# A gated cross-attention and expert layer on one Trainium2 core: first batch projected ahead of the branch, heads' products pinned

## The chip, the core and the metric

The kernel runs on one core of a Trainium2 chip. A core has TensorE (PE in the profile; PEld is its weight load), VectorE (DVE), ScalarE (ACT), GpSimd (POOL), and SyncE (SP), which here only issues transfers and waits for them. Transfers are issued by an engine into a queue and carried by 16 DMA engines. The metric is the device time of one execution in microseconds (us), with all inputs and outputs in the chip's memory. The time before is 850.95 us, the median of three runs (848.28 to 854.89).

## What is computed

The input x has 8 batches of 512 tokens of 256 numbers, the context likewise. Attention has 16 heads of 16 numbers. The feed-forward part has 8 experts with an inner size of 1,024; each token goes to its best two. The reference, cut to what matters:

```python
q = query @ wq.T + bq;  k = key @ wk.T + bk;  v = value @ wv.T + bv
scores = einsum('bhqd,bhkd->bhqk', q, k) / sqrt(16)
attn = softmax(where(mask == 0, -1e9, scores))
xattn = einsum('bhqk,bhkd->bhqd', attn, v) @ wo.T + bo
...
probs = softmax(x_flat @ router_w + router_b);  top_w, top_idx = top_k(probs, 2)
output += comb[:, e] * (gelu(x_flat @ expert_up[e].T) @ expert_down[e].T)   # for each expert e
...
x = x + tanh(g_xattn) * xattn(layernorm(x), ctx, ctx, mask)
x = x + tanh(g_ffn) * ffn(layernorm(x))
```

The mask is 512 x 512 integers, the same for all batches and heads. In the inputs drawn here every row is the same and keeps only the keys at the end, at most 128 of the 512.

## The kernel before

*Two branches, one mask.* The kernel handles any mask, but has a fast branch for masks whose kept keys lie within 128 neighbouring places, the same in every row. Whether that holds is found on the chip. The mask comes in four parts (L96 to L100, SP's queue). DVE turns each into 0 and 1 (`dropped`, L286), PE sums over the queries (`n_ps`, L292), DVE marks the keys that are kept (`act`, L293), and `most` (L298), a product and a maximum in one instruction, finds the first kept key, the end of the kept keys, and whether the rows differ (L303 to L305). From the first key comes the window's place `window_i`; from all three comes the flag `near_i` (L309 to L313). Then DVE makes, from the window, the matrix `pick` (L320 to L333) that PE uses to transpose the keys and blank those not kept, and the scaled biases `bks`, `bkm`, `bqs` and the value buffers `vals` (L336 to L349). All engines read `near_i` and branch (L1309); in the fast branch, `attend_near` (L718), SP also reads `window_i` (L741) and loads the window of the first two batches' context and the second batch's x.

*What is loaded when.* SP's queue takes x of batch 0 (L85), the mask, then the attention weights (L244 to L251). ACT's queue takes nine small inputs (L123 to L133): the two gates, five biases, the router's weights, and `bv` spread over all partitions. On DVE, small preparations (`iota_e` to `less`, L142 to L270) stand in the built order ahead of the comparisons with the mask; so does the first layernorm's statistics, `measure` (L207).

*One batch of attention.* Scores are made against 128 keys. The heads lie on partitions in pairs: 32 rows of a tile hold two heads of 16, and a tile of 128 rows holds four such pairs; there are two tiles, c = 0 and 1, and i = 0 and 1 chooses one of each pair. `k` holds the keys twice, with one head of each pair at zero (`half`), so that a product over 32 rows is one head's scores. The steps, for (c, i) = (0,0), (0,1), (1,0), (1,1), which are the four groups of a batch:
- `find_tops` (L834): eight products of 32 rows, `t_ps`, into four banks of PSUM; DVE takes each query's maximum over the keys.
- `lower_tops` (L851): PE transposes the maxima and DVE puts them, negated by way of `km`, into the spare rows of the queries (`lowered`, the tile `ql`).
- `weights_T` (L863): four products of 32 rows, one for each pair of heads, `w_ps`, into four banks; ACT takes the exponential into `pT`. This gives the softmax's weights with keys on partitions.
- `weigh` (L880): four products of 128 x 32 into one bank, `n_av`; DVE transposes and divides by the sums (L884 to L893).
- `project_out` (L900): the output projection, added to x.

`km` is the keys once more, with another bias (`bkm`, which is `bks` and `less` together) that puts -1 in the rows where the maxima come. Both `k` and `km` are made by ACT from the bank `k_ps` (L799 to L806), with four activations of 128 x 128 each.

*The order of the work.* Batch b's `weights_T` and `weigh` run beside batch b+1's `find_tops` and beside the preparation of batch b+2 (its projections `kv_ps`, `k_ps`, `q_ps`, L787 to L818), the layernorm statistics of batch b+3, and the routing of batch b-1. This is written out by hand. `between` (L915 and on) gives each step a place (g, n): group g of four, slot n of three. The loop over b from -1 to 7 runs the slots in order. A table (`amid`) puts the first experts' work into the slots of batches 4 to 7; the other experts' products follow, on PE alone. A tile scheduler decides how instructions that are not pinned to each other stand on an engine; `tc.keep_in_program_order` pins an instruction behind the last one before it in the program on its engine. In the built order of before, other instructions stand between the products of a group in 15 groups of `w_ps` and 7 of `t_ps`.

The statistics of batch 1 are computed ahead of the loop, those of batch 2 in the slots of b = -1. Buffers: four banks of PSUM for `t_ps` and `w_ps` (`ps_s`), two for projections and transposes (`bank`), two for `n_av`.

Of the kernel before, what the change touches and what calls it, by code (L numbers as in the profile page):

```python
# [10 lines left out]
F32 = mybir.dt.float32  # L11
I32 = mybir.dt.int32
# [7 lines left out]
P = 128  # L20
# [43 lines left out]
def flamingo_layer(ctx: ExitStack, tc: tile.TileContext, a: dict, out: bass.AP):  # L64
# [19 lines left out]
    def load_x(b, pool=keep):  # L84
        xs[b] = pool.tile([P, QT, D], F32, tag="x", name=f"x{b}", bufs=5 if b else 1)  # L85
        nc.sync.dma_start(out=xs[b], in_=token_rows(a["x"], b))


    load_x(0)
# [12 lines left out]
    mask_i = load_mask(mk)  # L102
    bq = fixed([P, DC], "bq")
# [18 lines left out]
    for dst, src in (  # L122
        (gates[:, 0:1], a["g_xattn"].partition_broadcast(P)),  # L123
        (gates[:, 1:2], a["g_ffn"].partition_broadcast(P)),
        (bk, a["bk"]),
        (bq, a["bq"]),
        (bvT, a["bv"].rearrange("(c p) -> p c", p=P)),
        (bo, a["bo"].partition_broadcast(P)),
        (rb, a["rb"].partition_broadcast(P)),
        (rw[:, :, :E], a["rw"].rearrange("(c p) e -> p c e", p=P)),  # L130
        (bv, a["bv"].partition_broadcast(P)),
    ):
        nc.scalar.dma_start(out=dst, in_=src)  # L133
# [10 lines left out]
    nc.scalar.activation(tg, gates, AF.Tanh)  # L144
# [99 lines left out]


    load_w("wqT")
    wkv = fixed([P, DC, 2 * D], "wkv")
    for i, n in enumerate(("wkT", "wvT")):
        nc.sync.dma_start(out=wkv[:, :, i * D : (i + 1) * D], in_=a[n].rearrange("(c p) d -> p c d", p=P))
        w[n] = wkv[:, :, i * D : (i + 1) * D]  # L250
    load_w("woT")  # L251

    own = fixed([P, 1], "own")
    tc.keep_in_program_order(nc.vector.tensor_copy(own, own_i))
    keys = mk.tile([P, S], F32, tag="keys", name="keys")
    tc.keep_in_program_order(nc.vector.tensor_copy(keys, keys_i))

    ahead = mk.tile([P, 2, S], F32, tag="ahead", name="ahead")
    tc.keep_in_program_order(nc.vector.tensor_scalar(ahead[:, 0, :], keys, -1.0, float(S), ALU.mult, ALU.add))
    tc.keep_in_program_order(nc.vector.tensor_scalar(ahead[:, 1, :], keys, 1.0, None, ALU.add))  # L260

    less = fixed([P, 2], "less")
    ident_j = ident.rearrange("p (j i) -> p i j", i=2 * DH)
    for i in range(2):
        tc.keep_in_program_order(nc.vector.tensor_reduce(less[:, i : i + 1], ident_j[:, DH * i, :], AX.X, ALU.add))
    tc.keep_in_program_order(nc.vector.tensor_scalar(less, less, -1.0, None, ALU.mult))  # L270

    act = mk.tile([P, S], F32, tag="act", name="act")
    first = fixed([P, 1], "first")
    window = fixed([P, 1], "window")
    window_i = fixed([P, 1], "window_i", I32)
    near_i = fixed([P, 1], "near_i", I32)
    with early, tc.tile_pool(name="ps_mask", bufs=1, space=PSUM) as ps_mask:

        def column(name, n=1):
            return mk.tile([P, n], F32, tag=name, name=name)  # L280

        dropped = mk.tile([P, QT, S], BF16, tag="dropped", name="dropped")
        norms_0 = measure(const, [(0, "a")], True)
        norms_0[1][0]()
        for t in range(QT):
            ins = nc.vector.tensor_scalar(dropped[:, t, :], mask_i[:, t, :], 0.0, None, ALU.is_equal)  # L286
            tc.keep_in_program_order(ins)
        norms_0[2]()

        n_ps = ps_mask.tile([P, S], F32, tag="n", name="n_ps")  # L290
        for t in range(QT):
            nc.tensor.matmul(n_ps, lhsT=ones_b, rhs=dropped[:, t, :], start=(t == 0), stop=(t == QT - 1))  # L292
        nc.vector.tensor_scalar(act, n_ps, float(S), None, ALU.is_lt)  # L293
        junk = column("junk", S)
        uneven, end = column("uneven"), column("end")

        def most(src, dst):
            nc.vector.tensor_tensor_reduce(  # L298
                junk, src, act, scale=1.0, scalar=0.0, op0=ALU.mult, op1=ALU.max, accum_out=dst
            )  # L300

        most(ahead[:, 0, :], first)
        nc.vector.tensor_scalar(first, first, -1.0, float(S), ALU.mult, ALU.add)  # L303
        nc.vector.tensor_scalar(window, first, float(S - WINDOW), None, ALU.min)
        tc.keep_in_program_order(nc.vector.tensor_copy(window_i, window))  # L305
        most(ahead[:, 1, :], end)
        most(n_ps, uneven)
        near = column("near")
        nc.vector.tensor_tensor(near, end, first, ALU.subtract)  # L309
        nc.vector.tensor_scalar(near, near, float(WINDOW), None, ALU.is_le)  # L310
        nc.vector.scalar_tensor_tensor(near, end, 1.0, near, ALU.is_ge, ALU.mult)
        nc.vector.scalar_tensor_tensor(near, uneven, 0.0, near, ALU.is_le, ALU.mult)
        tc.keep_in_program_order(nc.vector.tensor_copy(near_i, near))  # L313

        kept = fixed([P, 1], "kept")
        here = fixed([P, 1], "here")
        tc.keep_in_program_order(nc.vector.tensor_scalar(here, own, window, None, ALU.add))  # L320
        eq = column("eq", S)
        nc.vector.tensor_scalar(eq, keys, here, None, ALU.is_equal)
        nc.vector.tensor_tensor_reduce(eq, eq, act, scale=1.0, scalar=0.0, op0=ALU.mult, op1=ALU.max, accum_out=kept)
        diag = column("diag", P)
        nc.vector.tensor_scalar(diag, ident, kept, None, ALU.mult)
        row_ps = ps_mask.tile([P, P], F32, tag="row", name="row_ps")
        nc.tensor.matmul(row_ps, lhsT=ones, rhs=diag, start=True, stop=True)
        lead = fixed([P, 1], "lead")
        nc.vector.tensor_tensor(lead, here, first, ALU.is_equal)
        drop = column("drop", P)  # L330
        nc.vector.tensor_scalar(drop, row_ps, -1.0, 1.0, ALU.mult, ALU.add)
        pick = fixed([P, P], "pick")
        nc.vector.scalar_tensor_tensor(pick, drop, lead, diag, ALU.mult, ALU.add)  # L333


        vals = [fixed([P, H, 2 * DH], f"nv{i}") for i in range(3)]  # L336
        for t in vals:
            nc.vector.memset(t[:, :, DH:], 1.0)
            nc.vector.tensor_scalar(t[:, :, DH:], t[:, :, DH:], kept, None, ALU.mult)

        bks = fixed([P, 2, DC], "bks")
        for i in range(2):
            ins = nc.vector.tensor_scalar(bks[:, i, :], bk, half[:, 1 - i : 2 - i], None, ALU.mult)
            tc.keep_in_program_order(ins)
        bkm = fixed([P, 2, DC], "bkm")
        for i in range(2):
            nc.vector.tensor_scalar(bkm[:, i, :], bks[:, i, :], less[:, i : i + 1], None, ALU.add)
        bqs = fixed([P, DC], "bqs")
        tc.keep_in_program_order(nc.vector.tensor_scalar(bqs, bq, 1.0 / DH**0.5, None, ALU.mult))  # L349


    def shared(p2, small, bank):
# [145 lines left out]
        return layernorms, finish  # L498

# [219 lines left out]
    def attend_near(att):  # L719
# [18 lines left out]
        def held(shape, name, dtype=F32):  # L738
            return hold.tile(shape, dtype, tag=name, name=name)

        at = nc.values_load(  # L741
            window_i[0:1, 0:1], engines=(mybir.EngineType.SP,), min_val=0, max_val=S - WINDOW,
            skip_runtime_bounds_check_because="it is the lesser of the first key and S - WINDOW",
        )
        wins = {}

        def load_win(b):
            t = p2.tile([P, DC, WINDOW], F32, tag="win", name=f"win{b}", bufs=3)
            nc.sync.dma_start(
                out=t, in_=a["ctxT"][b].rearrange("(c p) s -> p c s", p=P)[:, :, bass.ds(at, WINDOW)]  # L750
            )
            wins[b] = t

        for b in range(2):
            load_win(b)
            if b == 0:
                load_x(1, p2)
# [14 lines left out]
        made = {}  # L772

        def prepare(b):

            xnT[b] = p2.tile([P, DC, S], F32, tag="xnT", name=f"n_xnT{b}", bufs=1)
            q = p2.tile([P, DC, S], F32, tag="q", name=f"n_q{b}")
            k = p2.tile([P, DC, 2, WINDOW], F32, tag="k", name=f"n_k{b}")
            km = p2.tile([P, DC, 2, WINDOW], F32, tag="km", name=f"n_km{b}")
            v = vals[b % 3]  # L780
            made[b] = (q, k, km, v)
            said = {}

            def keys_values():
                ps = bank(f"kv_ps{b}")
                for dc in range(DC):
                    nc.tensor.matmul(  # L787
                        ps, lhsT=wins[b][:, dc, :], rhs=wkv[:, dc, :], start=(dc == 0), stop=(dc == DC - 1)
                    )
# [590 lines left out]
```

## Time and profile before

One execution was profiled. It is a run of its own beside the three timed ones.

| | |
|---|---|
| median of three runs | 850.95 us |
| the profiled execution | 849.25 us |
| its span in the trace | 847.5 us |
| mean granted TensorE clock | 0.972 of full speed |
| moved in the span | 121.58 MB, 143 GB/s |

The page divides the span into 40 equal slices of 21.2 us; each digit is a share in tenths. In rows of a timeline the first number is the start in us from the span's start, the second the duration, then the engine, the line, the operation, the output tile and its inputs, the shape, and how many instructions the row holds; "[2.90 <-DMA mask_i]" says that the engine idled 2.90 us before and that a transfer into `mask_i` ended it. Slices further on look like this: from slice 5 to 19 attention on all engines, with the experts' first transfers; from about 400 us on, the expert products on PE with little beside them but ACT's gelu, and transfers.

```profile
ACT  0544464654455424352411011111112112111210
POOL 2002105252644232545464534444342523434332
DMA  4800011110482313061846566656567576657511
```

ACT and POOL are not full anywhere; DMA is busy in the first two slices, which hold the mask, x and the weights, and again in the experts' part.

### The profile page before, as it was taken

What the parts mean: (1) busy time and instruction counts of PE and PEld (TensorE: products, weight loads), DVE (VectorE), ACT (ScalarE), POOL (GpSimd) and SP (SyncE); (2) the same over time, 40 slices, a digit from 0 to 9 for tenths busy, and PEclk for the clock granted to TensorE, in tenths of its full rate; (3) what the DMA queues carried; (4) which work ended last, traced back from release to release, by engine and by line L of the source; (5) the groups of instructions that cost most, each with busy time, mean ns of one, the idle gap of its engine ahead of it and who ended that gap; (6) DMA issues with size and microseconds to landing.
All of it is one profiled execution on the core that took longest, in us unless ns stands there. A gap on an engine that the chain in (4) does not pass through costs nothing. (4 is left out here: it accounts for less than half of the span.)

```text
span 847.5 us, 11313 instructions
## 1 busy us (share of the span) xinstructions
PE 779.8 (92%) x4090; PEld 574.0 (68%) x4090; DVE 316.2 (37%) x960; ACT 259.4 (31%) x501; POOL 313.9 (37%) x422
## 2 busy tenths in 40 slices
PE   1698999999999899999999799999999999999992
PEld 0343444444356575767788588888898888989882
DVE  7367778787775628435230111111111111011110
ACT  0544464654455424352411011111112112111210
POOL 2002105252644232545464534444342523434332
PEclk9979999999799989999999899999999999999997
DMA  4800011110482313061846566656567576657511
GB/s 137 264 2 7 7 50 34 52 58 22 133 282 90 99 51 114 15 200 52 262 136 205 190 208 189 231 187 223 174 233 238 172 240 233 204 203 255 199 50 36
DMA packets 87909, 121.58 MB, mean 143 GB/s; under 512 B 16797, under 2 KB 71712, under 8 KB 87840
## 3 DMA queue, kind: packets, MB, share of 16 engines
q1 hardware_dynamic: 74448, 93.68, 33.3%
q0 software_dynamic: 11840, 26.76, 10.2%
q8 instruction: 36, 0.59, 0.3%
q10 hardware_dynamic: 1552, 0.28, 0.2%
q14 instruction: 33, 0.27, 0.1%
HBM read 101.05 MB, written 20.17 MB: 143 GB/s over the span
## 5 line engine op out<-in xcount | busy, mean ns | idle before, releaser
L665 PE MATMUL o_ps<-down,hT 128*128 128x256 f32 x1088 | 245.0, 384 | 6.5 <-DVE y L668 6.1
L647 PE MATMUL h_ps<-xT,up 128*128 128x256 f32 (+1 forms) x1152 | 246.6, 372 | 4.8 <-DVE tops L838 3.4
L647 PEld LDWEIGHTS h_ps<-xT,up 128*128 128x128 f32 x1152 | 210.7, 192 | 34.8 <-DVE tops L838 4.2
L665 PEld LDWEIGHTS o_ps<-down,hT 128*128 128x128 f32 x1088 | 206.4, 192 | 38.1 <-DVE y L668 6.3
L651 ACT ACTIVATE hT<-h_ps 128x512 f32<-128x512 f32 (+1 forms) x144 | 82.2, 573 | 363.0 <-PE h_ps L647 362.8
L668 DVE SCALAR_TENSOR_TENSOR y<-o_ps,listed,y 128x256 f32<-128x256 f32 x68 | 32.7, 483 | 277.6 <-DMA y<-out,listed 155.4
L619 POOL DMA_INDIRECT y<-out,listed x68 | 66.1, 972 | 163.1 <-DMA out<-y,listed 124.4
L671 POOL DMA_INDIRECT out<-y,listed x68 | 68.8, 1012 | 100.5 <-DVE y L668 70.5
L838 DVE TENSOR_REDUCE tops<-t_ps 128x4 f32<-128x512 f32 x128 | 79.3, 681 | 34.2 <-PE t_ps L834 34.2
L867 ACT ACTIVATE n_pT<-w_ps 128x512 f32<-128x512 f32 x128 | 70.0, 599 | 68.1 <-PE w_ps L863 68.0
L619 POOL DMA_INDIRECT xg<-rows,listed x68 | 64.9, 954 | 40.8 <-issue 17.4
L863 PE MATMUL w_ps<-ql,n_km 32*128 32x512 f32 x256 | 71.8, 667 | 2.5 <-DVE tops L838 2.5
L489 POOL DMA_INDIRECT table<-entries,place_i x64 | 62.5, 977 | 25.7 <-issue 16.5
L637 DVE COPY xT<-x_ps 128x512 f32<-128x512 f32 (+1 forms) x36 | 23.6, 656 | 101.4 <-PE x_ps L635 101.4
L834 PE MATMUL t_ps<-n_k,n_q 32*128 32x256 f32 x512 | 47.3, 411 | 2.0 <-ACT n_pT L867 1.2
L821 POOL TENSOR_TENSOR x<-x,bo 128x1024 f32<-128x1024 f32 x8 | 18.8, 2363 | 75.1 <-issue 38.8
L834 PEld LDWEIGHTS t_ps<-n_k,n_q 32*128 32x128 f32 x512 | 28.1, 188 | 24.2 <-issue 14.8
L814 PE MATMUL q_ps<-n_xnT,wqT 128*128 128x512 f32 x64 | 34.6, 667 | 6.2 <-ACT n_q L818 3.9
L863 PEld LDWEIGHTS w_ps<-ql,n_km 32*128 32x128 f32 x256 | 23.6, 189 | 21.0 <-DVE tops L838 14.5
L880 PE MATMUL n_av<-n_pT,nv 128*32 128x512 f32 x256 | 36.7, 630 | 0.0
L885 DVE STREAM_TRANSPOSE raw<-n_av 128x512 f32<-128x512 f32 x32 | 22.8, 712 | 35.2 <-PE n_av L880 35.2
L900 PE MATMUL proj_ps<-woT,oT 128*128 128x256 f32 x128 | 32.9, 392 | 1.6 <-DVE oT L893 1.6
(188 smaller groups left out, 547.2 us busy)
## 6 DMA issues: line engine op xcount, KB each, us to landing
up<-in_upT SPq DMA_DIRECT2D x36, 1024.0 KB, 7.7
down<-in_downT SPq DMA_DIRECT2D x36, 1024.0 KB, 6.3
x<-in_x SPq DMA_DIRECT2D x8, 512.0 KB, 4.9
out<-x SPq DMA_DIRECT2D x8, 512.0 KB, 3.0
rows<-xn_f SPq DMA_DIRECT2D x8, 512.0 KB, 3.8
table<-none SPq DMA_DIRECT2D x1, 2288.0 KB, 11.6
xg<-rows,listed POOLq DMA_INDIRECT x68, 3.9
y<-out,listed POOLq DMA_INDIRECT x68, 2.8
```

Of the source, the lines that this page charges most:

```text
L489: nc.gpsimd.indirect_dma_start(out=table_parts[2 * t + i][:, :], out_offset=bass.IndirectOffsetOnAxis(ap=place_i[:, t, i : i + 1], axis=0) ...
L619: nc.gpsimd.indirect_dma_start(out=dst, out_offset=None, in_=src[: seen[JOBS[s][0]], :], in_offset=bass.IndirectOffsetOnAxis(ap=listed[:, ...
L647: nc.tensor.matmul(ps[:, i, :n], lhsT=up[:, dc, (f + i) * P : (f + i + 1) * P], rhs=xT[:, dc, :n], start=(dc == 0), stop=(dc == DC - 1),)
L651: nc.scalar.activation(made[s][:, f : f + 2, :n], ps[:, :, :n], AF.Gelu)
L665: nc.tensor.matmul(ps, lhsT=hT[:, f, h * P : (h + 1) * P], rhs=down[:, f, :], start=(f == 0), stop=(f == FC - 1))
L671: nc.gpsimd.indirect_dma_start(out=out_parts[h][:, :], out_offset=bass.IndirectOffsetOnAxis(ap=listed[:, n, h, 0:1], axis=0), in_=y[:, h, ...
L814: nc.tensor.matmul(ps, lhsT=w["wqT"][:, dc, c * P : (c + 1) * P], rhs=xnT[b][:, dc, :], start=(dc == 0), stop=(dc == DC - 1),)
L834: nc.tensor.matmul(ps[j][:, u], lhsT=q[rows_j, c, t * P : (t + 1) * P], rhs=k[rows_j, c], start=True, stop=True)
L838: nc.vector.tensor_reduce(top[:, 2 * tp : 2 * tp + 2, :].rearrange("p t (i x) -> p t i x", i=2)[:, :, :, 32 * j], ps[j], AX.X, ALU.max,)
L863: nc.tensor.matmul(ps[j], lhsT=km[rows_j, c, i, :], rhs=lowered[b, c][rows_j, i, :], start=True, stop=True)
L867: nc.scalar.activation(pT[:, j, :], ps[j], AF.Exp)
L880: nc.tensor.matmul(av[32 * j : 32 * j + 32, :], lhsT=made[b][3][:, 8 * c + 2 * j + r, :], rhs=pT[:, j, :], start=True, stop=True,)
```

## The change

What it does, by parts:

1. Queues. The mask's four loads are the first on SP's queue; x of batch 0 goes to ACT's queue, with only `bk` and `bq` behind it. The seven other small loads go to SP's queue, behind the first window's load, pinned.
2. The mask's path. The first two comparisons are pinned ahead of the look at batch 0's statistics, the other two behind it. SP reads `window_i` as soon as it is made and loads the first window, ahead of `pick` and of the flag. `end`, `uneven` and `near_i` are computed behind `pick`, the biases and `vals[0]`. The zeros and ones of `vals` are set early.
3. Batch 0's projections (`kv_ps`, `k_ps`, `q_ps`), its scaling and its turns are made ahead of the branch, whatever the mask, with PSUM banks of their own. The window of batch 0 lives in the pool that is given back at the branch. `q`, `k` and `km` become two fixed buffers each, used in turn. The tanh of the gates moves behind these.
4. `km` is made from `k`, not from `k_ps`: two activations of 128 x 256 that add `less`, pinned, placed at slot (3,0).
5. The products of `t_ps`, `w_ps` and `n_av` are pinned, so that nothing stands between those of a group.
6. Statistics of batch 2 move from the slots of b = -1 to (0,0) and (0,1) of b = 0. `keys_values` of batch 1 moves from slot (0,0) to (0,2).

In the built order of after no group of `t_ps`, `w_ps` or `n_av` is cut; apart from the start, PE's instructions stand as before.

The diff, cut to its core (the pinning of `w_ps` and `n_av` reads like that of `t_ps`; the loops over loads name only the tiles):

```diff
-    def load_x(b, pool=keep):
+    def load_x(b, pool=keep, queue=nc.sync):
...
-        nc.sync.dma_start(out=xs[b], in_=token_rows(a["x"], b))
-    load_x(0)
+        queue.dma_start(out=xs[b], in_=token_rows(a["x"], b))
...
     mask_i = load_mask(mk)
+    load_x(0, queue=nc.scalar)
...
-    for dst, src in (gates, gates, bk, bq, bvT, bo, rb, rw, bv):
-        nc.scalar.dma_start(out=dst, in_=src)
+    nc.scalar.dma_start(out=bk, in_=a["bk"])
+    nc.scalar.dma_start(out=bq, in_=a["bq"])
...
-    nc.scalar.activation(tg, gates, AF.Tanh)
...
+        tc.keep_in_program_order(nc.vector.tensor_copy(window_i, window))
+        at = nc.values_load(window_i[0:1, 0:1], engines=(mybir.EngineType.SP,), ...)
+        win = load_window(mk, 0)
+        for dst, src in (gates, gates, bvT, bo, rb, rw, bv):
+            tc.keep_in_program_order(nc.sync.dma_start(out=dst, in_=src))
+        norms_0[2]()
...
+            def keys_less():
+                for i in range(2):
+                    ins = nc.scalar.activation(km[:, :, i, :], k[:, :, i, :], AF.Identity, bias=less[:, i : i + 1])
+                    tc.keep_in_program_order(ins)
...
+        def made_of(b):
+            return qs[b % 2], ks[b % 2], kms[b % 2], vals[b % 3]
+        xnT_0 = mk.tile([P, DC, S], F32, tag="xnT", name="n_xnT0")
+        _, scales, turns = shared(mk, const, bank_0)[0]([(0, "a", xnT_0)], True, norms_0)[2][0]
+        keys_values, keys_T, keys_less, queries = project(0, mk, bank_0, xnT_0, win)
+        for step in (*scales, keys_values, *turns, keys_T, *queries, keys_less):
+            step()
+        tc.keep_in_program_order(nc.scalar.activation(tg, gates, AF.Tanh))
...
-        for b in range(2):
-            load_win(b)
-            if b == 0:
-                load_x(1, p2)
+        load_win(1)
+        load_x(1, p2)
...
-                for dst, bias in ((k, bks), (km, bkm)):
-                    for i in range(2):
-                        for c in range(DC):
-                            nc.scalar.activation(dst[:, c, i, :], ps[...], AF.Identity, bias=bias[...], scale=half[...])
+                for i in range(2):
+                    for c in range(DC):
+                        nc.scalar.activation(k[:, c, i, :], ps[...], AF.Identity, bias=bks[...], scale=half[...])
...
-                    nc.tensor.matmul(ps[j][:, u], ...)
+                    ins = nc.tensor.matmul(ps[j][:, u], ...)
+                    tc.keep_in_program_order(ins)
...
-                put(0, 0, keys_values)
+                put(0, 2 if new == 1 else 0, keys_values)
                 put(0, 1, *scales)
                 put(1, 1, *turns, keys_T)
+                put(3, 0, keys_less)
...
+            if b == 0:
+                looks, settle = normalize((2, "a", lambda: xnT[2]))
+            plan = between(*(n if 0 <= n < B and (b, n) != (-1, 2) else None for n in (b - 1, b + 2, b + 3)))
+            if b == 0:
+                plan[0, 0] += looks
+                plan[0, 1].insert(0, settle)
```

## The prediction

> **What bounds the kernel now.** The page first: span, busy shares, slices.
>
> ```profile
> span 847.5 us, 11313 instructions
> PE 779.8 (92%) x4090; PEld 574.0 (68%) x4090; DVE 316.2 (37%) x960; ACT 259.4 (31%) x501; POOL 313.9 (37%) x422
> PE   1698999999999899999999799999999999999992
> PEclk9979999999799989999999899999999999999997
> ```
>
> TensorE is busy 92% of the span. Only the first slices are not full, and the clock row sags in a few. So two things can be won: the time before PE is full, and PE time that does no work. Next the timeline, all engines, from the start.
>
> ```profile
> 7.60 0.73 DVE L286 TENSOR_SCALAR dropped<-mask_i 128x512 bf16<-128x512 int32 x2
> ...
> 12.87 0.43 DVE L286 TENSOR_SCALAR dropped<-mask_i 128x512 bf16<-128x512 int32 x1 [2.90 <-DMA mask_i<-in_mask]
> ...
> 17.75 0.15 DVE L305 CAST window_i<-window 128x1 int32<-128x1 f32 x1
> ...
> 22.27 0.39 SPq L749 DMA_DIRECT2D win<-in_ctxT  x1
> ...
> 25.01 3.63 PE L787 MATMUL kv_ps<-wkv,win 128*128 128x512 f32 x4 [3.66 <-DMA win<-in_ctxT]
> ...
> 38.57 1.15 PE L834 MATMUL t_ps<-n_k,n_q 32*128 32x256 f32 x16
> ```
>
> A chain of waits: the last mask part (12.87), the window's place (17.90), the branch (22.27), the window's columns (25.01), batch 0's projections (38.57). Then PE's timeline in the steady state; a row is start, length, operation.
>
> ```profile
> 142.95 1.12 PE L863 MATMUL w_ps<-ql,n_km 32*128 32x512 f32 x2
> 144.00 0.71 PE L799 MATMUL k_ps<-pick,kn 128*128 128x128 f32 x4
> 144.55 0.60 PE L851 MATMUL top_ps<-ident,tops 128*128 128x128 f32 x4
> 145.08 1.13 PE L863 MATMUL w_ps<-ql,n_km 32*128 32x512 f32 x6
> 146.15 1.06 PE L880 MATMUL n_av<-n_pT,nv 128*32 128x512 f32 x8
> ```
>
> The two records of one head's 32-row product take 1.05 us (to 144.00), the six of the other three 1.07: heads on different rows run beside each other only while nothing stands between them. A whole group elsewhere:
>
> ```profile
> 248.84 1.14 PE L863 MATMUL w_ps<-ql,n_km 32*128 32x512 f32 x8
> 249.91 1.06 PE L880 MATMUL n_av<-n_pT,nv 128*32 128x512 f32 x8
> ```
>
> All four heads in 1.07. So a cut group costs 1.05 us more. Last, what would hold PE if these cuts went, from the view of stretches:
>
> ```profile
> 100.00:150.00 50.00, 48.08 (x314) 24.03 (x312) 42.28 (x129) 27.64 (x59) 13.62 (x23) 1.00 0.11 36
> ```
>
> Third is DVE: 42.28 of 50 us, against 48.08 on PE. It is the next bound, 6 us in 50 away.
>
> **The change part by part.** The sum stands against the profiled execution: 849.25 us, span 847.5. The median of the runs is 850.95, 1.7 above it.
>
> *Heads pinned.* The built order of PE has 15 cut groups of w_ps and 7 of t_ps before, none after; the rest of the order is the same but for the start. Gross: 15 x 1.05 = 15.8. A t_ps cut has its first part 0.63 (157.68 to 158.31) against 1.08 for a whole group: 7 x 0.63 = 4.4, and with four of them PE waits 0.35 for ACT's n_km: 1.4. In all 21.6. Net I walk one batch, 129.3 to 164.7 (35.4 us), which has three w_ps cuts and one t_ps cut. From 129 to 153.7 DVE is idle only 0.54, 0.36 and 0.36 us; PE can give back no more than that, and I take 1.1. From 153.7 to 160.1 DVE waits 1.46, 1.37 and 1.40 us for PE: there the cut at 153.39 (1.05) and the t_ps cut at 157.68 with its wait (0.63 + 0.35) come off entire, about 1.9. So 3.0 a batch. The bounds are 0 (DVE holds all) and 4.1 (gross). Three batches have three cuts: 9.0. Batches 0 and 1 have two each, with DVE less loaded: 1.5 each of 2.1, 3.0. The first group of batch 0 (cut by a bias product that waited 0.93): 0.5. Batch 5 has one w_ps and two t_ps cuts between expert products: 2.0. Together 14.5.
>
> *Keys for weights from those for maxima.* Four ACT reads of k_ps (1.52 us) become two of 128x256 in SBUF; that form is not in the trace. The 128x128 form takes 0.38, the 128x256 xn_a 0.52: 0.8 to 1.0 us for the two. ACT is 27.64 of 50 busy, so the 0.5 to 0.7 is worth nothing by itself; that these no longer stand between four exponentials is in the 1.9 above.
>
> *Mask alone on SP's queue.* Before, the third and fourth mask parts were issued only when small loads of ACT's queue had landed (SP's waits: 4.0 for gates, 1.4 for bq); the fourth was issued at 8.1 and landed 4.8 later. Now SP issues four in a row, about 0.45 apart, from 0.8. Before them and beside them go x0 and 1 MB of mask, 1.57 MB, from about 2.9; the trace moved 1.41 MB from 3 to 9 (235 GB/s) and 300 to 350 in full microseconds. So the last part lands between 7.4 and 9.6; I take 8.1, and the last comparison at 8.4 instead of 12.87. But in the built order DVE's preparations (iota_e to less, 2.31 to 6.4 in the trace, hidden under the mask) now stand behind the comparisons: 2.7 us of them (2.4 without waits, 4.0 as traced beside POOL's memsets) come before the window. From the last comparison to the window's end was 5.03; less the two other maxima moved behind (1.4), plus 2.7: 6.3 to 6.6. The window is ready at 15.0.
>
> *Projections ahead of the branch.* SP reads the register and issues win0 at 15.8 (0.4 to 1.3 later; SP came to its wait for pick, 2.2 us, at 20.07, 1.34 after near_i and two loads and a branch). It lands 2.7 later as traced: kv_ps at 18.5, not 25.01. The seven small loads queue on SP behind win0, some 4 us to 20, before near_i (about 22): hidden; tg waits for two of them, no more. From kv_ps to the last n_q was 12.64; without batch 1's xn_a, the four n_km and two short banks it is 3.63 + 1.0 (turns) + 1.1 (copies) + 3.8 (q_ps) + 0.7: 28.9. The new wait: in the branch win1 waits for PE's last q_ps (28.1), and x1 is issued behind it, at 28.6, where it was issued at 22.78. As traced it lands 4.1 later, 32.7. On DVE the stats of x1 stand ahead of the first tops, and PE's second t_ps and batch 1's turns wait for both. Tops end at 37.2 (42.2 before), xn_a of batch 1 at 42.0, its q_ps starts at 43.4 against 48.33: 4.9 won of the 9.7 that t_ps gained. Batch 2's stats and scaling (4.3 us of DVE, 42.13 to 48.42 between other work) now stand ahead of batch 1's first tops; DVE was idle 2.95 there, so 1.4 is lost. Net 3.5. Bounds: a loss of 1.0, if the mask comes no sooner; a gain of 5.5, if the half clock of 42.3 to 52.5 (q_ps 3.62 there, 1.98 later) falls in the wait.
>
> Sum: 849.25 - 3.5 - 9.0 - 3.0 - 0.5 - 2.0 = 831.25, say 831.
>
> **The rivals.**
>
> *DVE holds the batches.* The cuts filled time in which banks were read out; whole groups wait for the last bank instead. For it: 42.28 of 50, and tops of a group take 2.45 against PE's 1.07. Against it: the three idles of 4.23 us a batch. Then the cuts give 4, the start 2: 843. [...]
>
> *Everything comes off.* Gross 21.6 and 5.5 at the start: 822. It needs DVE to fill its idle time wholly.
>
> *The mask comes no sooner* (the change doesn't do what it says): x0 on ACT's queue shares the same 16 engines, and rates of 235 GB/s were seen. With the comparison at 12.87 the start is 4.5 worse than forecast: 836.
>
> *Slower: the clock.* The half clock came at 216.0, behind a PE idle of 1.62 us, and lasted 10.2; q_ps of four records then took 3.21 instead of 1.98. If whole groups bunch PE's idle time, each batch could set it off; a window costs 5.1. Four more eat the forecast's gain (831 + 20 = 851), six make 862. Against it: idles up to 1.39 at 150 set off nothing, and the change takes idle time away. [...]
>
> **How the numbers follow.** Forecast 0.60 (825 to 838), DVE 0.17 (839 to 848), everything off 0.12 (815 to 825), mask 0.05, clock 0.06. About 1% is what a measurement of this kernel tells from no change: 842.4 to 859.5 against 850.95. Faster: 0.60 + 0.12 + 0.05 and a fifth of the DVE case, 0.80; same: the rest of it, 0.14; slower: 0.06. The range 819 to 846 leaves out half of the gross case, the upper fifth of the DVE case and the clock: under 0.17.
>
> **What would show it.** The last comparison at 8 to 9.5, window_i at 14.5 to 16, the first kv_ps near 18.5, the first t_ps near 29 with tops only at 34: the start is right. If x1's landing is not what tops wait for, my new wait is wrong. No w_ps row of x2 or x6; a batch of 32.4 us; DVE's idle at PE's account near 2 a batch: the net price is right; at 34 us DVE holds it. More half-clock windows than five: the clock. The forecast is wrong if the first expert products come at another shift than the end, since the part from 400 us on, all PE, should only move.

## The result and the profile after

The changed kernel takes 830.71 us (median of four runs, 827.52 to 834.9); the kernel before takes 852.92 us beside it (four runs). The ratio is 0.974 (95% interval 0.969 to 0.979): 22 us less, or 2.6%. The forecast was 831 us. The total is right; of its terms the largest is not, as the runs below show.

The page of the changed kernel, profiled in an execution of 827.52 us:

```profile
span 825.8 us, 11292 instructions
...
PE 763.0 (92%) x4090; PEld 571.9 (69%) x4090; DVE 317.8 (38%) x958; ACT 252.6 (31%) x485; POOL 313.6 (38%) x422
...
PEclk9887999999999999999998999999999999999997
```

PE is busy 16.8 us less (779.8 before), and the span is 21.7 us shorter. The clock row sags at other places than before: in the second, third, fourth and 22nd slices, before in the third, 11th, 15th and 23rd (and in both kernels in the last).

The timeline at the start of the changed kernel:

```profile
17.52 3.75 PE L537 MATMUL kv_ps<-wkv,win 128*128 128x512 f32 x4 [0.48 <-DMA win<-in_ctxT]
...
27.45 1.15 PE L868 MATMUL t_ps<-k,q 32*128 32x256 f32 x16 [0.82 <-DVE groups L627]
...
31.44 0.75 DVE L209 BATCH_NORM_STATS2 st_a<-x 128x6 f32<-128x256 f32 x2 [4.10 <-DMA x<-in_x]
...
32.98 0.66 DVE L873 TENSOR_REDUCE tops<-t_ps 128x4 f32<-128x512 f32 x1
```

The first projection starts 7.5 us earlier (25.01 before), the first `t_ps` 11.1 us earlier (38.57). The first maxima are only 6.8 us earlier (39.73): DVE stands 4.10 us for batch 1's x, because its statistics come ahead of the maxima. Some 25 us later there is a second wait:

```profile
56.56 4.65 POOL L850 TENSOR_TENSOR x<-x,bo 128x1024 f32<-128x1024 f32 x2 [28.89 <-DVE bo L846]
...
58.17 0.76 DVE L217 TENSOR_SCALAR var_a<-mv_a 128x4 f32<-128x4 f32 x1
...
58.96 2.27 DVE L219 TENSOR_SCALAR rstd_a<-var_a 128x4 int32<-128x4 int32 x1
```

These two rows of 128 x 4 take 0.17 us elsewhere. Here they end at 58.93 and 61.23; POOL's two adds end at about 58.9 and 61.21. They are batch 2's statistics, which the change put ahead of batch 1's first maxima. PE then waits 3.58 us for the maxima (its next `w_ps` starts at 63.85) and gets half the clock up to about 74 (granted 0.53 from 63 to 74 us, 1.00 on both sides).

Where the 21.7 us lie, from the starts of the same operation in both traces (`kv_ps` of batch 4 is the start of the steady state; the last `lg_ps` is that of batch 7):

| stretch | before | after | gain | forecast |
|---|---|---|---|---|
| to the first `w_ps` | 57.57 | 55.28 | 2.3 | 3.5 |
| to `kv_ps` of batch 4 | 71.77 | 66.97 | 4.8 | 3.5 |
| to batch 5 | 35.36 | 33.20 | 2.2 | 3.0 |
| to batch 6 | 35.49 | 33.29 | 2.2 | 3.0 |
| to batch 7 | 41.13 | 36.32 | 4.8 | 3.0 |
| to the last `lg_ps` | 175.44 | 172.06 | 3.4 | 2.0 |
| to the end | 430.74 | 428.68 | 2.1 | 0 |

### The profile page after: what moved, and what is told of

Read it like the earlier page. It is cut to its first block, busy times and chain, and to the rows that moved or that the text cites. A ratio compares the mean times of both kernels' runs of the same rounds, so it can differ in the third digit from the quotient of the medians.

```text
span 825.8 us, 11292 instructions
## 1 busy us (share of the span) xinstructions
PE 763.0 (92%) x4090; PEld 571.9 (69%) x4090; DVE 317.8 (38%) x958; ACT 252.6 (31%) x485; POOL 313.6 (38%) x422
## 5 line engine op out<-in xcount | busy, mean ns | idle before, releaser
L755 DVE SCALAR_TENSOR_TENSOR y<-o_ps,listed,y 128x256 f32<-128x256 f32 x68 | 32.7, 483 | 271.6 <-DMA y<-out,listed 133.3
L903 ACT ACTIVATE n_pT<-w_ps 128x512 f32<-128x512 f32 x128 | 67.4, 598 | 44.4 <-PE w_ps L898 44.2
L898 PE MATMUL w_ps<-ql,km 32*128 32x512 f32 x256 | 62.8, 655 | 3.9 <-DVE tops L873 3.9
L868 PE MATMUL t_ps<-k,q 32*128 32x256 f32 x512 | 43.9, 416 | 3.0 <-DVE tops L873 2.2
L868 PEld LDWEIGHTS t_ps<-k,q 32*128 32x128 f32 x512 | 27.1, 191 | 25.3 <-issue 15.0
L898 PEld LDWEIGHTS w_ps<-ql,km 32*128 32x128 f32 x256 | 24.8, 187 | 19.7 <-DVE tops L873 15.0
L916 PE MATMUL n_av<-n_pT,nv 128*32 128x512 f32 x256 | 35.0, 619 | 0.0
L568 PE MATMUL q_ps<-n_xnT,wqT 128*128 128x512 f32 x64 | 32.9, 641 | 0.0
```

The source lines that it names most:

```text
L568: nc.tensor.matmul(ps, lhsT=w["wqT"][:, dc, c * P : (c + 1) * P], rhs=xnT[:, dc, :], start=(dc == 0), stop=(dc == DC - 1),)
L868: ins = nc.tensor.matmul(ps[j][:, u], lhsT=q[rows_j, c, t * P : (t + 1) * P], rhs=k[rows_j, c], start=True, stop=True)
L898: ins = nc.tensor.matmul(ps[j], lhsT=km[rows_j, c, i, :], rhs=lowered[b, c][rows_j, i, :], start=True, stop=True)
L903: nc.scalar.activation(pT[:, j, :], ps[j], AF.Exp)
L916: ins = nc.tensor.matmul(av[32 * j : 32 * j + 32, :], lhsT=made_of(b)[3][:, 8 * c + 2 * j + r, :], rhs=pT[:, j, :], start=True, stop=True,)
```

## The experiments

The theory on record: 14.5 us come from the pinned products, 3.5 from the start, and the keys' new source gives nothing by itself. The rivals: DVE holds the batches, so that pins give little; or the gain comes from another part. Each of these twelve kernels was timed against the kernel before on the same chip, in three groups of four. Only in the second group (km_only, km_pins, km_bank, km_bank_late) is the kernel before itself slower (868.0 us, where the other groups have 853.9 and 852.2), and in the traces of km_only, km_pins and km_bank_late batches 4 and 5 hold half-clock windows at 150 to 160 and 190 to 200 us (single stretches of 5 us there are granted as little as 0.61, 0.52 and 0.74); so times are read as ratios, and the batch that is compared across groups is the one from `kv_ps` of batch 3 to that of batch 4. There the granted clock is 1.00 in every trace of the table but that of pins_only (0.98). The trace of km_only is of its longest execution (862.42 us).

| kernel | us | before | ratio (95%) | that batch, us |
|---|---|---|---|---|
| before | | | 1 | 33.46 |
| the changed kernel | 830.71 | 852.92 | 0.974 (0.969 to 0.979) | 31.29 |
| pins_only | 854.76 | 853.89 | 1.001 (0.998 to 1.004) | 34.80 |
| no_pins | 837.11 | 853.89 | 0.979 (0.975 to 0.983) | 31.27 |
| stats_back | 832.32 | 853.89 | 0.975 (0.972 to 0.979) | 31.28 |
| bias_quarters | 830.05 | 853.89 | 0.972 (0.969 to 0.975) | 31.29 |
| km_only | 858.00 | 868.00 | 0.986 (0.980 to 0.992) | 31.29 |
| km_pins | 853.29 | 868.00 | 0.982 (0.976 to 0.988) | 31.27 |
| km_bank_late | 866.52 | 868.00 | 0.998 (0.994 to 1.001) | 34.61 |
| km_copy | 841.21 | 852.21 | 0.986 (0.982 to 0.990) | 31.29 |
| after_again | 832.49 | 852.21 | 0.976 (0.971 to 0.981) | 31.27 |
| x1_early | 825.69 | 852.21 | 0.968 (0.964 to 0.973) | 31.27 |
| start_three | 821.12 | 852.21 | 0.963 (0.959 to 0.968) | 31.30 |

### Pins alone, and all but the pins

pins_only is the kernel before with this, for `t_ps`, `w_ps` and `n_av`:

```diff
-                nc.tensor.matmul(
+                ins = nc.tensor.matmul(
                     ps[j], lhsT=km[rows_j, c, i, :], rhs=lowered[b, c][rows_j, i, :], start=True, stop=True
                 )
+                tc.keep_in_program_order(ins)
```

> The kernel before with nothing changed but the pinning of t_ps, w_ps and n_av: its built order has no cut group either. The forecast put 14.5 us of its 18.0 on the cut groups (9.0 in batches 2 to 4, 3.0 in batches 0 and 1, 0.5, 2.0), so by it the time is about 14.5 us below before, near 837, and a steady batch falls from 35.4 to 32.4 us. If DVE holds the batches, only 4 come off: near 847. If all comes off: 21.6, near 830. The trace of the change showed a steady batch of 33.2, 2.2 less and not 3.0, and 4.8 in the stretch of 200 to 241 us, where before had a half-clock window; if that window's end was luck, this kernel gains about 11.

Measured: 1.001. The pins alone give nothing (between 1.5 us won and 3.7 lost), and the compared batch gets longer, from 33.46 to 34.80, although no group is cut. The clock of 0.98 in it explains about 0.7 us (an estimate, 34.80 x 0.02); the next batch, at a clock of 1.00 in both traces, takes 36.04 us where the kernel before takes 35.36.

no_pins is the changed kernel without those three pins.

> The changed kernel with only the three pins taken out. Its built order has 9 cut groups of w_ps and 4 of t_ps, not the 15 and 7 of before: the keys' own move had already taken six cuts away. At the forecast's rate (14.5 for 21.6 gross) the 9 x 1.05 + 4 x 0.63 = 12.0 gross are 8 net: slower than the changed kernel by 8 us. If DVE holds the batches, 2 us. If the gain came from the start and not from the pins, no difference.

Measured: 0.979, some 2.5 to 4 us above the changed kernel's 0.974 and 0.976, with intervals that overlap. Its steady batches are 33.22 and 33.34 us, those of the changed kernel 33.20 and 33.29, although two groups of `w_ps` are cut in each. So the pins are worth nothing there. What is left of the difference need not be theirs: the profiled no_pins had a granted clock of 0.963, the profiled changed kernel 0.974, which is 9.5 us of full speed (837.0 x 0.037 less 825.8 x 0.026), and their spans differ by 11.2.

What takes a cut's place is seen in the changed kernel's steady batch: its last three groups of `w_ps` are whole, and take longer than the 1.07 us of a whole group that the prediction shows.

```profile
137.30 1.28 PE L898 MATMUL w_ps<-ql,km 32*128 32x512 f32 x8
...
144.96 2.79 PE L898 MATMUL w_ps<-ql,km 32*128 32x512 f32 x8
...
152.09 2.44 PE L898 MATMUL w_ps<-ql,km 32*128 32x512 f32 x8
```

### The keys, and the bank that they are read from

Why do pins alone make the batch longer? The view of one tile, `k_ps`, in pins_only (one batch; the starts of the first and last reader stand behind the durations), and who waited for its readers:

```profile
L806 ACT ACTIVATE n_k<-k_ps,bks,half x4: 448/457/462, 143.2 to 144.3; 128x128 f32<-128x128 f32 x4
L806 ACT ACTIVATE n_km<-k_ps,bkm,half x4: 472/482/490, 156.6 to 157.7; 128x128 f32<-128x128 f32 x4
...
  PE xnT_ps_f L376: 1.5, 1
```

`n_km` is not needed before the next batch, so it stands on ACT behind the exponentials, 12 us behind the last `n_k`. Until then it holds `k_ps`, one of the two PSUM banks that `q_ps`, `top_ps`, `xnT_ps` and the others share. These go through the one bank that is left: in that batch PE waits 1.69 and 0.78 us for ACT to read the queries out of it, and 1.51 for `n_km`.

```profile
150.62 1.98 PE L814 MATMUL q_ps<-n_xnT,wqT 128*128 128x512 f32 x4 [1.69 <-ACT n_q L818]
153.38 0.66 PE L852 MATMUL top_ps<-ident,tops 128*128 128x128 f32 x4 [0.78 <-ACT n_q L818]
...
158.20 0.66 PE L376 MATMUL xnT_ps_f<-ident,xn_f 128*128 128x128 f32 x4 [1.51 <-ACT n_km L806]
```

The kernel before has the same order, and waits less: 1.27 us for the queries and 0.35 for `n_km`. Its cut groups stand in part of that time.

```profile
151.48 1.98 PE L814 MATMUL q_ps<-n_xnT,wqT 128*128 128x512 f32 x4 [1.27 <-ACT n_q L818]
```

The view of `k_ps` in the kernel before:

```profile
L806 ACT ACTIVATE n_k<-k_ps,bks,half x4: 449/456/462, 144.8 to 145.8; 128x128 f32<-128x128 f32 x4
L806 ACT ACTIVATE n_km<-k_ps,bkm,half x4: 464/474/482, 157.2 to 158.2; 128x128 f32<-128x128 f32 x4
```

and of the changed kernel, in which `k_ps` has one kind of reader and is free 2.3 us after its product starts, not 14.7:

```profile
L555 ACT ACTIVATE k<-k_ps,bks,half x4: 450/456/463, 137.0 to 138.0; 128x128 f32<-128x128 f32 x4
```

That made a new theory (A in what follows): the keys' move wins because it frees a bank, not because it saves ACT time. km_only and km_pins are the kernel before and pins_only with this:

```diff
-                for dst, bias in ((k, bks), (km, bkm)):
-                    for i in range(2):
-                        for c in range(DC):
-                            nc.scalar.activation(dst[:, c, i, :], ps[...], AF.Identity, bias=bias[...], scale=half[...])
+                for i in range(2):
+                    for c in range(DC):
+                        nc.scalar.activation(k[:, c, i, :], ps[...], AF.Identity, bias=bks[...], scale=half[...])
...
+            def keys_less():
+                for i in range(2):
+                    ins = nc.scalar.activation(km[:, :, i, :], k[:, :, i, :], AF.Identity, bias=less[:, i : i + 1])
+                    tc.keep_in_program_order(ins)
...
+                put(3, 0, keys_less)
```

> The kernel before with one thing changed: km is made from k by two 128x256 activations at slot (3,0), pinned, and not from k_ps; t_ps, w_ps and n_av are not pinned, the start is as before. The forecast gave this part nothing by itself, and pins_only shows that the pins alone give nothing. Theory A (the k_ps bank, one of two for projections and transposes, is held until the last n_km has read it, and q_ps, top_ps and xnT_ps queue behind the one other bank): a steady batch falls from 35.4 to about 33.2 us, the total by 8 to 12. Rival B (the gain needs pins and keys together): the batch stays at 35 or more.

> km_only with t_ps, w_ps and n_av pinned as well: the changed kernel without its new start. What the pins add to km_only is 0 to 3 us by theory A (batches of 33.2 us in both), 8 or more by the forecast's pricing. What then lies between this kernel and the changed one is the start's worth: 3.5 us by the forecast, 6 to 9 by what is left over if the keys give 8 to 12.

Measured: 0.986 and 0.982. The compared batch falls from 33.46 to 31.29 by the keys alone, and pins leave it at 31.27. The keys are worth 1.4%, some 12 us of 852.9 (7 to 17 by the interval). What pins add, 0.4%, is inside the intervals, and so is the start's worth if it is taken from these ratios (0.982 to 0.974 and 0.976, across groups). The expected steady batch of 33.2 isn't to be had from these two traces: from batch 4 on they have 38.3 to 38.5, with a wait in which PE, ACT and DVE all stand (1.44 us on PE to 147.24 in km_pins) and half a clock behind it (granted 0.54, 0.50 and 0.50 from 150 to 156). What makes it was not found.

The bank by itself: in the changed kernel, `km` is again made from `k_ps`. In km_bank the activations stand right behind those of `k`; in km_bank_late they stand at (3,0), where the changed kernel makes `km`:

```diff
+                said["k_ps"] = ps
...
             def keys_less():
+                ps = said["k_ps"]
                 for i in range(2):
-                    ins = nc.scalar.activation(km[:, :, i, :], k[:, :, i, :], AF.Identity, bias=less[:, i : i + 1])
-                    tc.keep_in_program_order(ins)
+                    for c in range(DC):
+                        ins = nc.scalar.activation(km[:, c, i, :], ps[...], AF.Identity, bias=bkm[...], scale=half[...])
+                        tc.keep_in_program_order(ins)
```

> The changed kernel with km again made from k_ps, by four 128x128 activations; in the built order they stand right behind those of k, ahead of the exponentials, so the bank is free some 1.5 us later than in the changed kernel, and not some 20 us later as in pins_only. Theory A (only the bank's holding time matters): batches of 33.2 to 33.6, total within 2 us of the changed kernel. Rival B (ACT's time, or the form, matters): batches of 35 and more, 8 us slower.

> km_bank with the four activations of km moved to slot (3,0), pinned behind the last exponentials, the place where the changed kernel makes km: the same work, but the k_ps bank is held for some 13 to 20 us. Theory A: q_ps, top_ps and xnT_ps wait as in pins_only, batches of 35.5 to 37.5, total 8 to 15 us above km_bank. Rival B: as km_bank.

km_bank tells nothing: with two buffers, early keys of batch b+2 go into the buffer that batch b's last two groups still have to read, so these two groups take the wrong batch's keys, and new waits arise (912.64 us, ratio 1.052). A version with a third buffer was not tried. km_bank_late gives 0.998: the whole gain of the keys is gone, and with it what the start had won. Its compared batch is 34.61. The view of `k_ps`, whose bank is now held for 18.5 us (143.6 to 162.1):

```profile
L560 ACT ACTIVATE k<-k_ps,bks,half x4: 450/458/465, 144.4 to 145.4; 128x128 f32<-128x128 f32 x4
L569 ACT ACTIVATE km<-k_ps,bkm,half x4: 482/493/502, 160.5 to 161.6; 128x128 f32<-128x128 f32 x4
```

km_copy keeps those late activations, and takes the bank away from them:

```diff
-                said["k_ps"] = ps
+                nc.scalar.copy(said["kn"], ps[:, :D])
...
-                ps = said["k_ps"]
+                ps = said["kn"]
```

> km_bank_late with one thing more: ACT copies k_ps into SBUF (the buffer of kn, no longer needed) right ahead of k, and the four late activations of km read that copy. So ACT does 0.4 us more a batch than in km_bank_late, at the same places, and only the time for which the k_ps bank is held differs. Theory A (the bank's holding is what costs): the batches come back to about 33.2 us and the total to the changed kernel's, 15 to 20 us below km_bank_late. Rival B (the four activations at that place cost it): as km_bank_late, no better than before.

The view of `k_ps` in km_copy:

```profile
L560 ACT ACTIVATE k<-k_ps,bks,half x4: 459/466/473, 139.5 to 140.5; 128x128 f32<-128x128 f32 x4
L557 ACT COPY kn<-k_ps x1: 372/372/372, 139.2 to 139.2; 128x256 f32<-128x256 f32 x1
```

The bank is free 2.6 us after its product starts (138.4). The late activations take as long as before, 0.50 us each where km_bank_late has 0.49.

Measured: batches of 31.29, 33.20 and 33.31 us, those of the changed kernel to a hundredth or two, with more work on ACT than any other kernel of the table (260.5 us; the kernel before has 259.4). Theory A stands. Its second half doesn't: the total is 841.21, halfway, not the changed kernel's. The spans differ by 9.8 us (842.0 and 832.2 in after_again), and the clock gives nearly that (842.0 x 0.042 less 832.2 x 0.031 = 9.6). Of the 9.8 us 5.3 lie between `kv_ps` of batch 7 and the last `lg_ps`. Why this kernel met more half clock was not found; so a part of the ratio of km_bank_late may be clock as well, but not its batch of 34.61, which lies at a clock of 1.00.

### The start

after_again is the changed kernel, run once more as the measure for its group.

> The changed kernel itself, once more, beside the other three of this group on one chip: they are measured against it. Ratio to before 0.974, as in its first four runs.

Measured: 0.976, and batches as in the first profile. The part behind the last `lg_ps`, where the code is the same in all kernels, took 434.57 us in this profile and 428.68 in the first: so the 2.1 us that the table above shows there are less than what two executions of one kernel differ by.

stats_back undoes the move of batch 2's statistics:

```diff
-            if b == 0:
-                looks, settle = normalize((2, "a", lambda: xnT[2]))
-            plan = between(*(n if 0 <= n < B and (b, n) != (-1, 2) else None for n in (b - 1, b + 2, b + 3)))
-            if b == 0:
-                plan[0, 0] += looks
-                plan[0, 1].insert(0, settle)
+            plan = between(*(n if 0 <= n < B else None for n in (b - 1, b + 2, b + 3)))
```

> The changed kernel with batch 2's statistics back among the steps of b = -1. In the changed kernel's trace those statistics stand ahead of batch 1's first maxima, two TENSOR_SCALAR rows of them took 0.76 and 2.27 us beside POOL's adds of the bias, and PE idled 3.58 us at 60 to 64 us. Theory A (the moved statistics ate the start's gain): that wait goes, 2 to 4 us faster. Rival B: the statistics now wait for batch 2's x, which is issued late, and hold batch 0's maxima instead: no faster, or up to 3 us slower.

bias_quarters cuts POOL's adds:

```diff
-            nc.gpsimd.tensor_tensor(xs[b], xs[b], bo.unsqueeze(1).to_broadcast([P, QT, D]), ALU.add)
+            for t in range(QT):
+                nc.gpsimd.tensor_tensor(xs[b][:, t, :], xs[b][:, t, :], bo, ALU.add)
```

> The changed kernel with POOL's add of the bias, one instruction of 128x1024 a batch, cut into four of 128x256; the same sums. Theory A (two instructions of DVE waited until POOL's running add had ended, at 58.93 and 61.23 us): the two rows shorten to about 0.6 us each, PE's wait of 3.58 us falls by about 2, and the time by about 2 us. Rival B (those rows were long for another reason): rows and time stay.

stats_back: parts of both A and B happen. The first `w_ps` is 1.6 us later (56.85), the second group 2.1 us earlier (61.77, where the changed kernel has 63.85), the first `lg_ps` 1.1 us earlier. The time shows no difference (0.975 beside 0.974 and 0.976).

bias_quarters: the two rows shorten to 0.51 and 0.65 us, as expected if an instruction of DVE waits for the running add of POOL. But the next four small instructions of the chain (60.03 to 62.72) now take 0.65 us each as well, one for each quarter, PE's wait stays at 3.64 us, and the time shows no difference (0.972). So the cause was right and the cure wrong: POOL's work is no shorter than before (5.50 us, where the two whole adds take 4.65), and a chain of ten dependent instructions meets each piece. Not all of DVE's rows wait: beside the adds TENSOR_SCALAR and TENSOR_TENSOR rows of 128 x 4 take up to 2.27 and 0.64 us instead of 0.17 and 0.16, BATCH_NORM_STATS2 rows 0.40 each, as elsewhere. What makes the difference was not shown.

x1_early takes batch 1's x out of the branch:

```diff
     load_w("woT")
+    load_x(1, tag="x1")
...
         load_win(1)
-        load_x(1, p2)
...
-                load_x(b + 3, p2)
+                if b == 3:
+                    xs[6] = xs[1]
+                    nc.sync.dma_start(out=xs[6], in_=token_rows(a["x"], 6))
+                else:
+                    load_x(b + 3, p2, bufs=4)
```

> The changed kernel with the second batch's x loaded into a buffer of its own behind the weights on SP's queue, ahead of the mask's result, and not in the branch behind the window that waits for the last q_ps. (Batch 6's x takes that buffer later, and four buffers are left where five were.) In the changed kernel DVE idled 4.10 us for x1 and took the first maxima at 32.98, 5.5 us behind the first t_ps. Theory A (x1's landing holds the start): first maxima at 28 to 29, first w_ps some 4 us earlier, time 2 to 4 us lower. Rival B (batch 2's statistics, POOL's adds and the clock take it back): first maxima earlier, but the time within 1.5 us of the changed kernel.

Measured: 825.69 us, 6.8 less than after_again (0.968 and 0.976). DVE's rows in its timeline:

```profile
21.42 0.75 DVE L209 BATCH_NORM_STATS2 st_a<-x 128x6 f32<-128x256 f32 x2 [0.32 <-issue]
...
30.45 2.48 DVE L873 TENSOR_REDUCE tops<-t_ps 128x4 f32<-128x512 f32 x4
```

The look at batch 1's x now lies in DVE's idle time beside the projections, and the maxima come in one row, at 30.45 (28 to 29 expected, 32.98 in the changed kernel). The first `w_ps` starts at 47.05, 8.2 us ahead of the changed kernel's 55.28. That is twice the 4 expected, though the maxima won only 2.5: the rest goes with the half clock. From 35 to 50 us the changed kernel is granted 0.60, 0.50 and 0.87 in three stretches of 5 us, x1_early 1.00, and the first `q_ps` of batch 1 takes 1.92 us instead of 3.62. The half clock now comes at 55 to 65 (granted 0.50 and 0.55). The wait at 55.63 (3.59 us, for the statistics beside POOL) is still there.

start_three adds the edit of stats_back and this:

```diff
+    vals = [fixed([P, H, 2 * DH], f"nv{i}") for i in range(3)]
+    for t in vals:
+        nc.vector.memset(t[:, :, DH:], 1.0)
     own = fixed([P, 1], "own")
...
-    vals = [fixed([P, H, 2 * DH], f"nv{i}") for i in range(3)]
-    for t in vals:
-        nc.vector.memset(t[:, :, DH:], 1.0)
```

> x1_early with two more edits: the memsets of vals ahead of own in the program, so that DVE's preparations come ahead of the comparisons again (2.7 us less between the last comparison and the window), and batch 2's statistics back among the steps of b = -1. If the three add up: window_i at 11.5 to 12 and not 14.26, first t_ps near 25, first w_ps 6 to 9 us earlier than in the changed kernel, time 5 to 8 us lower. If DVE or the half clock behind longer waits of PE takes it back: within 2 us of it.

Measured: 821.12 us, 11.4 less than after_again, 3.7% less than the kernel before (0.963). `window_i` is made at 11.95 (14.26), the first `t_ps` starts at 25.07, the first `w_ps` at 45.46, 10 us earlier than in after_again (55.53), and the first `lg_ps` 12.1 us earlier. The time was expected to fall by 5 to 8 us; how the 11.4 divide between the half clock and each of the three edits was not measured. This is the fastest version found.

## Why the prediction was right, and where it wasn't

- *The total* was right by luck, because errors cancelled. The step that failed is "Heads pinned": 14.5 us in all, priced from the cut groups. Alone the pins give nothing (1.001), and taken out of the changed kernel they leave a steady batch as it is (33.22 and 33.20). Luck has a second part: the forecast took its 18 us off the profiled execution (849.25), and the measured 22 come off a median of 852.92.
- *The step on the keys* failed with it. It counted ACT's time (1.52 against some 0.9 us) and found it worth nothing. The runs show some 12 us, by way of what those reads hold: a PSUM bank for 14.7 us instead of 2.3. The forecast had named that `n_km` stands between four exponentials, and that PE waits 0.35 for it; it did not ask which tile stays taken as long as it hasn't run. PE's waits for ACT's `n_q` in the same batch (1.27 us at 151.48) were the sign of it, and were not followed.
- *The walk through a batch* gave 3.0; measured 2.2 a batch. The place was right: the time came off between 153 and 160 us, where DVE waits. But the built order of no_pins shows that the `w_ps` cut and the `t_ps` cut there go away with the keys' move, pins or no pins. In the first two thirds nothing came off, as DVE's 0.36 to 0.54 of idle time said. DVE's idle time on PE's account, which should have come to near 2 us a batch, is 3.4 (from 122.25 to 155.45; 5.5 before). The rows of whole groups show what takes a cut's place: `w_ps` of eight records takes 1.28, 2.79 and 2.44 us in one batch, as its banks come free, not 1.07.
- *The third steady batch* gained 4.8, which is about the half-clock window (216.0 to 226.2 at a granted 0.51, some 5 us) that the kernel before had in this execution and the changed one not; the step gave it no price.
- *The start*: each row came within 1.5 us of the forecast, and all but the first earlier (last comparison 8.4 as forecast, window 14.4 for 15.0, `kv_ps` 17.52 for 18.5, first `t_ps` 27.45 for 28.9, to which the terms that are given add up only as 28.7, x1 31.4 for 32.7, `q_ps` of batch 1 42.28 for 43.4). The new wait for x1 is real, and with the half clock behind it (granted 0.60, 0.50 and 0.87 from 35 to 50 us) was the larger part of what was lost: x1_early wins 6.8 us. The term that was mis-sized is batch 2's statistics: 1.4 us forecast, 4.5 measured (at the `t_ps` of 57.41 the changed kernel leads by 6.2, at the `w_ps` of 63.85 by 1.7), of which 2.7 are the two rows beside POOL's adds, a meeting that the forecast didn't look for. That all of the 4.5 is theirs isn't shown: from the first `w_ps` group to the second stats_back takes 3.7 us less than the changed kernel (4.92 and 8.57), and starts the first 1.6 later.
- *The rivals.* "DVE holds the batches" was nearly right on the pins (4 us by it, none measured) and wrong on the total, since the gain had another source. "Everything comes off" (822) is out, and so is "The mask comes no sooner". The half clock did decide several microseconds, in both directions (some 5 us won in the third steady batch; a granted 0.53 from 63 to 74 us in the changed kernel's start) and from one execution to the next (by an estimate from span and clock, 832.2 x 0.031 less 825.8 x 0.026, 4.3 of the 6.4 us between two executions of the changed kernel).

## What to carry to other kernels

When a reader of a PSUM bank is moved or dropped, price the time for which the bank stays taken, not the reader's own time: 1.5 us of reads that could come late cost some 12 us here, since everything else went through the other bank. A cut in a group cost nothing here, where the engine would have waited for a bank anyway; look for the wait first. And when a transfer is issued behind a wait, ask who stands for it; here SP waited 5.5 us for the last `q_ps` before it issued x1, and moving that one load ahead of the wait won 6.8 us, over half of the keys' gain, in part by the half clock that it took away (1.00 granted from 35 to 50 us, where the changed kernel has 0.50 to 0.87).

## What the hardware showed that was not expected

- The same kernel, profiled twice, had spans of 825.8 and 832.2 us at granted clocks of 0.974 and 0.969; 5.9 of the 6.4 us lie behind the last `lg_ps`, where both run the same instructions.
- In these traces idle time of PE doesn't tell by itself when the half clock comes: 1.62 us at 215 us came ahead of it in the kernel before (granted 0.51 from 216.0 to 226.2), 1.27 us at 150, where the prediction has 1.39, did not (granted 1.00 from 140 to 165), nor did 2.21 us at 204.49 in the changed one (granted 1.00 from 200 to 215).
- Cutting an instruction of POOL into four let DVE's chain in between, but six small instructions in a row took 0.51 to 0.65 us each instead of 0.16, as long in all as beside the two whole adds (3.7 us).
